# Layer 2's attention block: one store per head for the first block's turned sums, a fetch split by heads, and the last norm's offset added to x

## The chip, the core and the metric

The kernel runs on one core of one Trainium2 chip. The metric is the device time of one execution in microseconds (us). A core has five queues of instructions that matter here: TensorE (PE, matmuls, with its weight loads as PEld), VectorE (DVE), ScalarE (ACT), GpSimd (POOL) and SyncE (SP). SP computes nothing: it issues the DMA transfers. Each queue is worked through in order, and a queue stands while its first instruction waits.

## What is computed

The program is a network of four layers on x of shape (4, 128, 64, 64): four batches of 128 channels and 4096 positions. Layer 0 is a convolution with a state-space scan, layer 1 a 3x3 convolution, layer 2 an attention block and a mixture of experts, layer 3 a linear attention and another mixture of experts. The change lies in layer 2's attention block alone. Its reference, cut to what matters (`t` is x as 4096 tokens of 128 values, 16 heads of 8):

```python
def _L2_attn_ref(x, ...):
    qkv = _qz_ring(heads + rx_theta)              # products of cosines
    q = jnp.transpose(qkv, (0, 2, 1, 3))
    scores = jnp.einsum('bhsd,bhtd->bhst', q, q) / np.sqrt(D)
    attn = jax.nn.softmax(scores, axis=-1)
    ctx = jnp.einsum('bhst,bhtd->bhsd', attn, q)
    ...
    attn_out = ctx @ w_comb.T + b_comb
    x1 = _ln(x + attn_out, g1, beta1)
    zf = jnp.cos(x1[..., :NQ_FFN]) * jnp.cos(ry_theta)
    h = jax.nn.relu(zf @ w1.T + b1)
    ffn_out = h @ w2.T + b2
    return _ln(x1 + ffn_out, g2, beta2)
...
t = t + _L2_attn_ref(_ln_t(t), ...)
```

Queries, keys and values are one array, so the matrix of scores is symmetric.

## The kernel before

**Stages.** `layer2_attention` works on one batch after another. For batch b it runs a stage that mixes two jobs, `feed_forward(b - 1)` and `prepare(b)`, and then `attention(b)`. Before the first attention there is only a preparation, after the last only a feed-forward. So there are four attentions and four stages that hold a feed-forward. Between a stage and an attention the on-chip buffers are given up and taken anew: the first writes of the next stage can't start before the last readers of the old buffers are done.

**Order.** In `attention` the order on PE, DVE and POOL is the order in which the code is written. In the mixed stages the compiler's scheduler orders every queue, from its own estimates of durations; the order in the code is only a priority. `in_turn` gives that priority: in turn i it calls the last step for chunk i - 9, the step before it for chunk i - 8, and so on back to the first step for chunk i.

**Attention.** The 4096 queries are cut into four blocks j of 1024. Because of the symmetry, the exponentials of only some pairs of blocks are computed: block j meets the key blocks `meets[j]` from ((1, 2), (2, 3), (3,), (0,)), and its own. A pair's exponentials serve twice: upright in `weigh`, where PE sums them into `ctx_ps` for the queries of block j, and turned by DVE (L1401, L1425), where `turn` sums them into `accs[h][:, i]` for the queries of the met block i (L1309, L1311). For blocks 1 to 3 these turned sums are added into `ctx_ps` before `weigh` copies the block out (L1353) and stores numerators and denominators by head (L1358, L1359). Block 0 is finished first, while its turned sums come from block 3, at the head's end. They therefore go to memory on their own: `around_d`. On chip such a sum has 128 rows: row 32 g + 8 a + d is the g-th of four partial sums, for quarter a of each run of 128 tokens, and dimension d of the head. Columns are (t, r): token 128 t + 32 a + r. In L1315 to L1321 each of the sixteen groups of 8 rows (g, a) is stored by a DMA of its own, so that `around_d[g]` is in the order of dimensions and tokens.

**Feed-forward.** Ten steps per chunk of 512 tokens, in the order of chunks 2 to 7, then 0 and 1: `fetch` (loads of den, num, nrm_in, and for chunks 0 and 1 of `around`), `divisors`, `attended`, `first_centred`, `first_norm`, `cosines`, `hidden`, `sum_up`, `last_centred`, `last_norm`. `divisors` adds the four parts of `around` into num on POOL (L1465, L1466). `sum_up` also requests the x chunk (L1517), to which `last_norm` adds the block's result on POOL (L1534) before it is stored (L1535). x has three buffers. Both norms run through `layernorm_steps`: after the square on ACT (L105) come a matmul of means, a transpose, square root, reciprocal and transpose, a multiplication by the gain on DVE (L120) and the addition of the offset on POOL (L121). The buffer of `around` shares the tag "hid" with the hidden layer's, two buffers in all.

**Preparation.** `prepare` norms the chunk, stores it (`nrm_d`, L1131), computes the products of cosines on DVE, ACT and POOL (L1152, L1154, L1156), and stores values and heads (`value_d` L1170, `head_d` L1184). At its end `load(0)` issues 32 loads (L1097) of queries and keys for the first head, which POOL rounds (L1106).

Of the kernel before, what the change touches and what calls it, by code (L numbers as in the profile page):

```python
# [9 lines left out]
F32 = mybir.dt.float32  # L10
# [3 lines left out]
ALU = mybir.AluOpType  # L14
# [3 lines left out]
P = 128  # L18
NB = 4
HW = 64  # L20
L = HW * HW
CH = 512
# [7 lines left out]
class Common:  # L30
# [58 lines left out]
    def mm(self, out, lhsT, rhs, start=True, stop=True):  # L89
        self.nc.tensor.matmul(out, lhsT, rhs, start=start, stop=stop)  # L90
# [8 lines left out]
    def layernorm_steps(self, out, src, work, psum, g=None, b=None, tag="mm", bufs=None):  # L99

        nc = self.nc
        xc = psum.tile([P, CH], F32, name="ln_xc", tag=tag, bufs=bufs)
        self.mm(xc, self.center, src)
        sq = work.tile([P, CH], F32, name="ln_sq", bufs=bufs)
        nc.scalar.activation(sq, xc, AF.Square)  # L105
        yield
        vp = psum.tile([P, CH], F32, name="ln_var", tag="mm")
        self.mm(vp, self.mean, sq)
        vt = work.tile([P, CH // 32, 32], F32, name="ln_vt")
        nc.vector.transpose(vt.rearrange("p a b -> p (a b)"), vp)  # L110
        sd = work.tile([P, CH // 32, 1], F32, name="ln_sd")
        nc.scalar.activation(sd, vt[:, :, 0:1], AF.Sqrt, bias=self.eps5)
        nc.vector.reciprocal(sd, sd)
        rs = work.tile([P, CH // 32, 32], F32, name="ln_rs")
        nc.vector.transpose(rs, sd.to_broadcast([P, CH // 32, 32]))  # L115
        rs = rs.rearrange("p a b -> p (a b)")
        if g is None:
            nc.vector.tensor_tensor(out, xc, rs, ALU.mult)  # L118
        else:
            nc.vector.scalar_tensor_tensor(rs, xc, g, rs, ALU.mult, ALU.mult)  # L120
            nc.gpsimd.tensor_scalar(out, rs, b, None, ALU.add)  # L121
# [105 lines left out]
def column(nc, pool, v, name, n=1, p=P):  # L227

    t = pool.tile([p, n], F32, name=name)
    nc.sync.dma_start(out=t, in_=v.rearrange("(n p) -> p n", p=p))  # L230
    return t
# [786 lines left out]
def layer2_attention(K, xd, dpool, w):  # L1018

    nc, tc, mm = K.nc, K.tc, K.mm  # L1020
    NH, HD = 16, 8
    NJ = 4
    BT = NTT // NJ
    scale = 1.0 / math.sqrt(HD)
    with ExitStack() as ctx:
# [8 lines left out]
        g2 = column(nc, cst, w["g2"], "g2")  # L1034
        beta2 = column(nc, cst, w["beta2"], "beta2")
# [7 lines left out]
        for k in range(4):  # L1043
            r = slice(32 * k, 32 * k + HD)
# [29 lines left out]
        value_d = dpool.tile([NH, 32, NJ, 4, BT, HD], F32, name="value_d")  # L1074
        num_d = dpool.tile([2, P, L], F32, name="num_d")
        den_d = dpool.tile([2, NH, L], F32, name="den_d")
        around_d = dpool.tile([4, P, L // NJ], F32, name="around_d")
        nrm_d = [dpool.tile([P, L], F32, name=f"nrm_d{i}") for i in range(2)]

        unit = lambda p, c: slice(32 * (2 * p + c), 32 * (2 * p + c) + 32)  # L1080
# [118 lines left out]
        def attention(qt, first, dsum, big, two, work, pssc, psctx, psacc):  # L1199
# [56 lines left out]
            for k, (h, j, i) in enumerate(order):  # L1256
                at = fills[h, j, i][-1] + 3
# [20 lines left out]
            accs = {}  # L1278
# [4 lines left out]
            def turn():  # L1283

                r, h, j, i, td, sums = groups[0]
                if r == 0:
                    sums = groups[0][-1] = aps[:, halves[0] % 2]
                    halves[0] += 1
                groups[0][0] += 1
                tv = values[h, j]  # L1290
                for g in range(4):
                    n = 4 * r + g
                    q, t = divmod(n, BT)
                    at = 32 * (4 * t + q)
                    mm(
                        sums[32 * g : 32 * g + 32],
                        tv[:, n].rearrange("p a d -> p (a d)"),
                        td[:, :, at : at + 32],
                        start=r == 0,
                        stop=r == BT - 1,  # L1300
                    )
                if r < BT - 1:
                    return
                groups.pop(0)
                if h not in accs:
                    accs[h] = work.tile([P, NJ, BT, 32], F32, name="acc")
                at = accs[h][:, i]
                if j == from_[i][0]:
                    nc.vector.tensor_copy(at, sums)  # L1309
                else:  # L1310
                    nc.vector.tensor_tensor(at, at, sums, ALU.add)  # L1311
                if i == 0:


                    for g in range(4):  # L1315
                        for a in range(4):
                            rows_ = slice(32 * g + HD * a, 32 * g + HD * a + HD)
                            nc.sync.dma_start(
                                out=around_d[g, HD * h : HD * h + HD].rearrange("d (t a r) -> d t a r", a=4, r=32)[:, :, a],
                                in_=accs[h][rows_, 0],  # L1320
                            )  # L1321
                if i == meets[j][-1]:
                    waiting.append(now[0] + 2)

# [52 lines left out]
            for n, (h, j, m) in enumerate(steps):  # L1377
# [10 lines left out]
                i = m // 4  # L1388
# [16 lines left out]
                for _ in range(rounds[n]):  # L1405
                    turn()

                while folds and (folds[0][0] <= n and not behind or len(folds) > 5):
                    _, qs, at = folds.pop(0)
# [3 lines left out]
                if behind:  # L1413
                    sums = dacc[:, from_[i].index(j), h]
                for p in range(2):
                    ex = exs[:, p]
                    t = 2 * m + p
# [25 lines left out]
        def feed_forward(b, dsum, work, psum):  # L1443

            CHB = NCH // NJ
            loads, x1s, hids, sums, halves, lasts, rcs, arounds = {}, {}, {}, {}, {}, {}, {}, {}

            def fetch(c):
                cols = slice(c * CH, (c + 1) * CH)
                den = work.tile([2 * NH, CH], F32, name="den", bufs=3)  # L1450
                nc.sync.dma_start(out=den, in_=den_d[:, :, cols].rearrange("p h f -> (p h) f"))
                num = work.tile([P, 2, CH], F32, name="num", bufs=2)
                nc.sync.dma_start(out=num, in_=num_d[:, :, cols].rearrange("p q f -> q p f"))
                nrm = work.tile([P, CH], F32, name="nrm_in", bufs=4)
                nc.sync.dma_start(out=nrm, in_=nrm_d[b % 2][:, cols])
                if c < CHB:
                    part = arounds[c] = work.tile([P, 4, CH], F32, name="around", tag="hid")
                    nc.sync.dma_start(out=part, in_=around_d[:, :, cols].rearrange("g q f -> q g f"))
                loads[c] = num, den, nrm

            def divisors(c):
                num, den, at = loads[c]
                if c in arounds:
                    part = arounds.pop(c)
                    nc.gpsimd.tensor_tensor(part[:, 0:2], part[:, 0:2], part[:, 2:4], ALU.add)  # L1465
                    nc.gpsimd.tensor_tensor(num, num, part[:, 0:2], ALU.add)  # L1466

                tp = psum.tile([P, 4, 2 * NH], F32, name="den_t", tag="mm")
                for j in range(4):
                    nc.tensor.transpose(tp[:, j, :], den[:, j * P : (j + 1) * P], K.ident[0 : 2 * NH, 0 : 2 * NH])  # L1470
                rd = work.tile([P, 4, NH], F32, name="rd")
                nc.vector.tensor_reduce(rd, tp.rearrange("p j (z h) -> p j h z", z=2), AX.X, ALU.add)
                nc.vector.tensor_tensor(rd, rd, dsum[:, 4 * c : 4 * c + 4], ALU.add)
                nc.vector.reciprocal(rd, rd)
                rc = rcs[c] = work.tile([P, 4, NH, HD], F32, name="rc")
                nc.vector.tensor_copy(rc, rd.unsqueeze(3).to_broadcast([P, 4, NH, HD]))
# [36 lines left out]
                    nc.scalar.activation(hid[:, k, :], hps[k], AF.Relu, bias=b1[:, k : k + 1])  # L1513

            def sum_up(c):
                x = loads[c] = work.tile([P, CH], F32, name="x", bufs=3)
                nc.sync.dma_start(out=x, in_=xd[b][:, c * CH : (c + 1) * CH])  # L1517
                hid = hids[c]
                fp = psum.tile([P, CH], F32, name="ffn_ps", tag="mm")
                for k in range(4):  # L1520
                    mm(fp, w2T[:, k, :], hid[:, k, :], start=k == 0, stop=k == 3)
                r = sums[c] = work.tile([P, CH], F32, name="res")
                nc.vector.scalar_tensor_tensor(r, fp, b2, x1s[c], ALU.add, ALU.add)

            def last_centred(c):
                sums[c] = sums[c], work.tile([P, CH], F32, name="blk")
                lasts[c] = K.layernorm_steps(sums[c][1], sums[c][0], work, psum, g2, beta2, tag="xc", bufs=3)
                next(lasts[c])

            def last_norm(c):  # L1530
                next(lasts.pop(c), None)
                o = sums[c][1]
                x = loads[c]
                nc.gpsimd.tensor_tensor(x, x, o, ALU.add)  # L1534
                nc.sync.dma_start(out=xd[b][:, c * CH : (c + 1) * CH], in_=x)  # L1535
# [6 lines left out]
        for b in range(NB + 1):  # L1542
            with (
# [3 lines left out]
                with (  # L1547
# [4 lines left out]
                    if b < NB:  # L1552
                        part, qt, first = prepare(b, big, two, work, psum)
# [448 lines left out]
```

## Time and profile before

| what | us |
|---|---|
| median of 3 runs | 10257.94 (10254.08 to 10261.23) |
| the profiled execution's own time | 10257.22 |
| its span | 10255.4 |
| PE / DVE / ACT / POOL busy | 8783.8 / 7559.2 / 7455.2 / 4791.2 |
| layers 0 and 1, up to about | 2970 |
| attentions, about | 3116 to 4416, 4630 to 5934, 6149 to 7450, 7664 to 8950 |
| expert layers and layer 3, from about | 9100 |

The profile is one execution. A line of its timeline gives the start in us, the duration in us, the engine, the source line, the operation, and output<-input; x16 at the end means that sixteen such instructions in a row were merged. In square brackets stands how long the engine had been idle before it, and what ended the wait. SPq is SP's queue, where a DMA line is the issue, not the transfer. L90 is the helper through which nearly all matmuls are recorded, L110 to L121 are `layernorm_steps`, and L215 to L224 the cosine; for them the names of the tiles say which step it is. Over the whole span the DMA engines move 60 GB/s on average, and 193592 of the 631668 packets are under 512 B.

### The profile page before, as it was taken

Reading aid. Unit: us, or ns where it says so; the run is one execution under the profiler, and the core shown is the slowest. Engines: PE = TensorE matmul, PEld = TensorE weight load, DVE = VectorE, ACT = ScalarE, POOL = GpSimd, SP = SyncE. Lnnn points to the kernel's source line nnn. Section 1 sums busy time; section 2 is a strip of 40 time slices with the busy share of each in tenths; the row PEclk is TensorE's granted clock in tenths of the full one; section 3 lists DMA queues with packets and bytes.
Section 4 is the critical chain, followed back from the end, with each engine's and each line's share of the span. In section 5 each row is a group of like instructions: output and inputs, shape, how many; then the busy total and the mean of one; then the engine's idle time right before and its main releaser. Section 6 shows DMA issues by size and latency. Waiting matters only on the chain. (4 is left out here: it accounts for less than half of the span.)

```text
span 10255.4 us, 186421 instructions
## 1 busy us (share of the span) xinstructions
PE 8783.8 (86%) x72472; PEld 3322.6 (32%) x72472; DVE 7559.2 (74%) x8247; ACT 7455.2 (73%) x10632; POOL 4791.2 (47%) x3135
## 2 busy tenths in 40 slices
PE   6777777778868999979999969999969999967766
PEld 2222222224442333333333323333323333323433
DVE  1888788887846888877888868888868888753563
ACT  2666666664438999969999959999959999831531
POOL 1666676665524555545555545555545555420000
PEclk9787877888989999989999989999989999988988
DMA  3332423322212222232222132222142222123004
GB/s 81 98 79 69 103 68 97 76 61 73 79 62 48 38 39 39 37 98 42 40 39 42 32 104 38 40 43 39 29 111 35 42 38 40 34 95 117 0 18 148
DMA packets 631668, 617.44 MB, mean 60 GB/s; under 512 B 193592, under 2 KB 425088, under 8 KB 629760
## 3 DMA queue, kind: packets, MB, share of 16 engines
q1 hardware_dynamic: 630784, 605.51, 25.3%
q8 instruction: 572, 9.37, 0.4%
q14 instruction: 312, 2.56, 0.1%
HBM read 394.93 MB, written 91.23 MB: 47 GB/s over the span
## 5 line engine op out<-in xcount | busy, mean ns | idle before, releaser
L1419 ACT ACTIVATE ex<-score 128x1024 f32<-128x1024 f32 x5120 | 4927.2, 1037 | 175.0 <-PE score L90 89.5
L90 PE MATMUL ctx_ps<-ex,qt 128*32 128x512 f32 x20480 | 2735.0, 606 | 19.7 <-DVE ctx L1353 19.7
L1368 POOL TENSOR_TENSOR folded<-ex 128x1024 f32<-128x1024 f32 x512 | 1224.3, 2391 | 2123.2 <-ACT ex L1419 1853.4
L1425 DVE STREAM_TRANSPOSE turned<-ex 128x1024 f32<-128x1024 f32 x1536 | 1885.5, 1228 | 373.2 <-ACT ex L1419 295.8
L1401 DVE STREAM_TRANSPOSE turned<-ex 128x1024 f32<-128x1024 f32 x1532 | 1842.2, 1203 | 0.0
L90 PE MATMUL acc_ps<-turned,turned_v 128*32 128x256 f32 x24576 | 1769.5, 379 | 3.0 <-DVE turned L1431 3.0
L90 PE MATMUL score<-queries,keys 32*128 32x512 f32 x10240 | 1333.9, 497 | 93.8 <-ACT ex L1419 45.5
L829 DVE TENSOR_TENSOR_SCAN hs<-decay,carry,hs 128x512 f32<-128x512 f32 x1024 | 1246.0, 1264 | 181.7 <-ACT decay L825 167.7
L825 ACT ACTIVATE decay<-dt,a_neg 128x512 f32<-128x512 f32 x1024 | 692.8, 688 | 820.5 <-DVE hs L829 798.0
L90 PEld LDWEIGHTS acc_ps<-turned,turned_v 128*32 128x32 f32 x24576 | 800.9, 110 | 1476.4 <-issue 1327.1
L833 POOL TENSOR_TENSOR hs<-hs,c_sb 128x1024 f32<-128x1024 f32 x512 | 1209.4, 2362 | 60.5 <-DMA c_sb<-c_d 19.6
L90 PEld LDWEIGHTS score<-queries,keys 32*128 32x128 f32 x10240 | 512.6, 182 | 1190.5 <-ACT ex L1419 819.0
L1225 POOL TENSOR_TENSOR turned_v<-v,quarter 128x1024 f32<-128x1024 f32 x256 | 612.5, 2393 | 265.4 <-PE acc_ps L90 209.7
L90 PE MATMUL y_ps<-hs,pair 128*64 128x512 f32 x2048 | 673.2, 785 | 48.9 <-POOL hs L833 48.5
L818 DVE TENSOR_TENSOR hs<-dtx,b_ps 128x2048 f32<-128x2048 f32 x256 | 579.7, 2265 | 176.3 <-DMA dtx<-dtx 132.9
L1369 POOL TENSOR_TENSOR quarters<-folded 128x512 f32<-128x512 f32 x512 | 658.1, 1285 | 40.1
L90 PE MATMUL b_ps<-dbc,state 32*64 32x512 f32 x1024 | 342.8, 751 | 385.5 <-DVE hs L818 385.1
L90 PEld LDWEIGHTS ctx_ps<-ex,qt 128*32 128x32 f32 x20480 | 406.4, 108 | 654.7 <-issue 598.8
L832 POOL COPY carry<-hs 128x2 f32<-128x2 f32 x512 | 96.3, 188 | 897.0 <-DVE hs L829 847.0
L1419 ACT ACTIVATION_READ_ACCUMULATOR ex<-score 128x1 f32 x2048 | 437.2, 213 | 0.0
L1353 DVE COPY ctx<-ctx_ps 128x512 f32<-128x512 f32 x256 | 176.9, 691 | 328.9 <-PE ctx_ps L90 307.8
L1410 DVE TENSOR_REDUCE dacc<-quarters 128x2 f32<-128x512 f32 x508 | 327.0, 644 | 0.0
(358 smaller groups left out, 9384.2 us busy)
## 6 DMA issues: line engine op xcount, KB each, us to landing
c_sb<-c_d SPq DMA_DIRECT2D x512, 128.0 KB
queries<-head_d SPq DMA_DIRECT2D x1024, 64.0 KB
keys<-head_d SPq DMA_DIRECT2D x1024, 64.0 KB
dt<-dt SPq DMA_DIRECT2D x128, 256.0 KB
dtx<-dtx SPq DMA_DIRECT2D x128, 256.0 KB
v<-value_d SPq DMA_DIRECT2D x1024, 32.0 KB
w<-in_L_ffn_weight SPq DMA_DIRECT2D x32, 1024.0 KB
w<-in_L_ffn_weight SPq DMA_DIRECT2D x128, 256.0 KB
```

What stands on the lines that cost most here:

```text
L90: self.nc.tensor.matmul(out, lhsT, rhs, start=start, stop=stop)
L818: nc.vector.tensor_tensor(hs, dtx2, bb.unsqueeze(1).to_broadcast([P, NQ, CH]), ALU.mult)
L825: nc.scalar.activation(ex, dt2[:, q, :], AF.Exp, scale=a_neg[:, q, g : g + 1])
L829: nc.vector.tensor_tensor_scan(hs[:, q, :], decays[q - 2 * i], hs[:, q, :], carry[:, g, q : q + 1], ALU.mult, ALU.add)
L833: nc.gpsimd.tensor_tensor(hs[:, two, :], hs[:, two, :], cs.unsqueeze(1).to_broadcast([P, 2, CH]), ALU.mult)
L1225: nc.gpsimd.tensor_tensor(t, v.unsqueeze(2).to_broadcast([P, 4 * BT, 4, HD]), quarter.unsqueeze(1).to_broadcast([P, 4 * BT, 4, HD]), ALU.mult,
L1368: nc.gpsimd.tensor_tensor(hs, exs[:, :, 0], exs[:, :, 1], ALU.add)
L1369: nc.gpsimd.tensor_tensor(qs, hs[:, :, 0 : CH // 2], hs[:, :, CH // 2 :], ALU.add)
L1401: nc.vector.transpose(*upright)
L1410: nc.vector.tensor_reduce(at, qs, AX.X, ALU.add)
L1419: nc.scalar.activation(ex, sps[p], AF.Exp, scale=scale, accum_out=sums[:, t : t + 1] if summed else None)
L1425: nc.vector.transpose(*upright)
```

## The change

Four edits:

- In `turn`, the turned sums of block 0 are stored by one DMA per head, rows and columns as they stand on chip; `around_d` has a part for each head.
- In `fetch`, `around` is loaded by 16 DMAs, one per head, each to that head's 8 rows; the sixteen (g, a) groups now lie side by side in a row. `divisors` adds groups 8 to 15 onto 0 to 7, then each half of the result onto the matching half of num, whose columns are read and written in the order (a, t, r).
- `layernorm_steps` gets a third form: with a gain and no offset, DVE writes the product to the result, and POOL's addition is left out. The last norm uses it.
- The request of the x chunk goes from `sum_up` to `last_centred`, the next step, behind that step's own instructions, and POOL adds the offset beta2 to x there.

```diff
@@ layernorm_steps
         if g is None:
             nc.vector.tensor_tensor(out, xc, rs, ALU.mult)
+        elif b is None:
+            nc.vector.scalar_tensor_tensor(out, xc, g, rs, ALU.mult, ALU.mult)
         else:
@@ layer2_attention
-        around_d = dpool.tile([4, P, L // NJ], F32, name="around_d")
+        around_d = dpool.tile([NH, P, L // NJ // 4], F32, name="around_d")
@@ turn
                 if i == 0:
-                    for g in range(4):
-                        for a in range(4):
-                            rows_ = slice(32 * g + HD * a, 32 * g + HD * a + HD)
-                            nc.sync.dma_start(
-                                out=around_d[g, HD * h : HD * h + HD].rearrange("d (t a r) -> d t a r", a=4, r=32)[:, :, a],
-                                in_=accs[h][rows_, 0],
-                            )
+                    nc.sync.dma_start(out=around_d[h], in_=accs[h][:, 0].rearrange("p t r -> p (t r)"))
@@ fetch
-                    part = arounds[c] = work.tile([P, 4, CH], F32, name="around", tag="hid")
-                    nc.sync.dma_start(out=part, in_=around_d[:, :, cols].rearrange("g q f -> q g f"))
+                    part = arounds[c] = work.tile([P, 16, P], F32, name="around", tag="hid")
+                    for h in range(NH):
+                        nc.sync.dma_start(
+                            out=part[HD * h : HD * h + HD],
+                            in_=around_d[h, :, c * P : (c + 1) * P].rearrange("(n d) f -> d n f", d=HD),
+                        )
@@ divisors
-                    nc.gpsimd.tensor_tensor(part[:, 0:2], part[:, 0:2], part[:, 2:4], ALU.add)
-                    nc.gpsimd.tensor_tensor(num, num, part[:, 0:2], ALU.add)
+                    nc.gpsimd.tensor_tensor(part[:, 0:8], part[:, 0:8], part[:, 8:16], ALU.add)
+                    for i in range(2):
+                        at = num[:, i].rearrange("p (t a r) -> p a t r", a=4, r=32)
+                        more = part[:, 4 * i : 4 * i + 4].rearrange("p a (t r) -> p a t r", r=32)
+                        nc.gpsimd.tensor_tensor(at, at, more, ALU.add)
@@ sum_up
-                x = loads[c] = work.tile([P, CH], F32, name="x", bufs=3)
-                nc.sync.dma_start(out=x, in_=xd[b][:, c * CH : (c + 1) * CH])
@@ last_centred
-                lasts[c] = K.layernorm_steps(sums[c][1], sums[c][0], work, psum, g2, beta2, tag="xc", bufs=3)
+                lasts[c] = K.layernorm_steps(sums[c][1], sums[c][0], work, psum, g2, tag="xc", bufs=3)
                 next(lasts[c])
+                x = loads[c] = work.tile([P, CH], F32, name="x", bufs=3)
+                nc.sync.dma_start(out=x, in_=xd[b][:, c * CH : (c + 1) * CH])
+                nc.gpsimd.tensor_scalar(x, x, beta2, None, ALU.add)
```

## The prediction

> **What bounds the kernel now.** I read, in this order, the page's costliest groups, the busy time by stage, and the timeline where one stage of layer 2's attention hands over to the next.
>
> ```profile
> L1419 ACT ACTIVATE ex<-score 128x1024 f32<-128x1024 f32 x5120 | 4927.2, 1037 | 175.0 <-PE score L90 89.5
> 3116.00:4416.00 1300.00, 1280.68 (x14586) 451.37 (x14586) 1038.40 (x1057) 1236.96 (x1792) 676.39 (x352) 0.99 0.21 37
> 4416.00:4630.00 214.00, 138.26 (x422) 63.62 (x422) 153.42 (x288) 117.39 (x173) 95.26 (x102) 0.81 0.42 122
> ```
>
> The first line is the exponential, 4927 us over four batches. The other two are one batch's attention and the stage behind it (columns: window, length, busy time and count of PE, weight loads, DVE, ACT, POOL; clock; DMA share; GB/s). In attention ACT works 1237 of 1300 us. Its waits in that window are 22.9 us on PE's scores, 11.7 us without a recorded cause and 3.6 us on POOL; none is on a DMA. The stores of the turned sums are therefore hidden while attention runs, and taking them away there brings nothing. In the 214 us stage no engine is near full (PE 138, DVE 153): it is a chain of waits with idle ends. The four feed-forward stages are where the change acts. This is the end of attention 0:
>
> ```profile
> 4403.21 0.42 DVE L1309 COPY acc<-acc_ps 128x256 f32<-128x256 f32 x1 [3.29 <-PE acc_ps L90]
> 4403.66 11.53 SPq L1318 DMA_DIRECT2D around_d<-acc  x16
> 4404.26 1.86 DVE L1441 TENSOR_REDUCE dsum<-dacc 128x512 f32<-128x1024 f32 x1
> 4416.78 0.33 SPq L1451 DMA_DIRECT2D den<-den_d  x1
> 4419.20 0.60 PE L1470 MATMUL den_t<-ident,den 32*128 32x32 f32 x4 [16.06 <-DMA den<-den_d]
> 4424.87 0.60 ACT L105 ACTIVATE ln_sq<-ln_xc 128x512 f32<-128x512 f32 x1 [27.98 <-DMA nrm_in<-nrm_d]
> ```
>
> The last head's turned sums are copied at 4403.2. SP then issues sixteen stores in 11.5 us, and the first load of the next stage (den) leaves only at 4416.78; the view of SP's waits gives its last 1.3 us to "DMA around_d<-acc". Compute is done at 4406.1 (DVE dsum), yet PE idles 16.06 us and ACT 27.98 us. Nothing covers this gap.
>
> The other end of the stage, where attention 1 starts:
>
> ```profile
> 4616.24 6.11 SPq L1535 DMA_DIRECT2D xd<-x  x3
> 4623.11 0.45 SPq L1517 DMA_DIRECT2D x<-xd  x1
> 4626.75 1.26 POOL L1534 TENSOR_TENSOR x<-x,blk 128x512 f32<-128x512 f32 x1 [4.75 <-DMA x<-xd]
> 4628.04 0.32 SPq L1535 DMA_DIRECT2D xd<-x  x1
> 4630.40 1.28 ACT L1419 ACT_TABLE_LOAD   x1 [15.61 <-DMA xd<-x]
> ```
>
> The eighth x chunk is requested at 4623.11, because its buffer is free only after an earlier chunk's store, and SP stands in three stores until 4622.35. It arrives, is added at 4626.75, stored at 4628.04, and ACT, idle for 15.61 us, starts when that store has landed. Last, what follows a fetch:
>
> ```profile
> 3081.71 11.04 SPq L1097 DMA_DIRECT2D keys<-head_d  x16
> 3099.77 1.89 POOL L1106 CAST keys<-keys 128x2048 fp32r<-128x2048 f32 x1 [21.23 <-DMA queries<-head_d]
> ...
> 9015.66 0.37 SPq L1458 DMA_DIRECT2D around<-around_d  x1
> 9020.78 2.36 POOL L1465 TENSOR_TENSOR around<-around 128x1024 f32<-128x1024 f32 x1 [3.80 <-DMA around<-around_d]
> ...
> 4501.21 1.60 POOL L1484 TENSOR_TENSOR num<-num 128x512 f32<-128x512 f32 x1
> 4538.09 0.64 DVE L1485 TENSOR_TENSOR num<-num,rd_ps 128x512 f32<-128x512 f32 x1
> ```
>
> Sixteen 64 KB key loads of 8 partitions in 512 B rows, which is exactly the new fetch's form, are usable 18.1 us after the first issue; today's single 1 MB fetch is usable 5.1 us after its issue here (6.4 us in the first fetch of that stage, 8.4 us at 4519.55). In the last pair the chunk that needs the first fetch is ready on POOL at 4502.8, and DVE takes it up at 4538.1.
>
> **What the Trainium skill says.** "DMA: Bandwidth & Descriptors", section "Why a DMA increments its semaphore by 16 and not by 1": a DMA runs on as many engines, up to 16, as divide the slowest dimension of both sides; 8 partitions get at most 8. The trace agrees in direction: 68 GB/s over the key loads (3081.7 to 3099.8), 253 GB/s over the stretch after the fetch at 4489.1. [...] The x store at 4628.04 releases ACT 2.36 us later, its issue included[...]. "GPSIMD Engine Reference", section "Performance pitfalls for Q7 kernels": reads slow down when the inner step passes 8 bytes. The new adds step 4 bytes in runs of 32, so I price them like today's; no row of before has that form.
>
> **The change, part by part.** The sum is against the profiled execution, 10257.2 us (span 10255.4), which is within 1 us of the median 10257.9.
>
> 1. *Stores.* 1024 issues become 64. In attention, hidden as said: 0. At the four ends, from first store to first den load: 4403.66 to 4416.78 = 13.1; 5919.54 to 5932.19 = 12.65; 7438.67 to 7451.18 = 12.5; 8953.97 to 8966.70 = 12.7; together 51.0 us. Now one store takes about 0.35 to issue (head_d's, of 128 partitions too, 0.38) and 2.0 to land, like the x store. DVE's dsum ends 2.46 us after the first store, so both finish together and each gap shrinks to 2.5. Gain 51.0 - 10.0 = 41 us. Late next is den's own load (2.4 us, as now). If the store lands late like the 3.6 us x load, the gain is 36.
>
> 2. *Fetch by heads.* Per batch two fetches; each puts 16 issues on SP (keys: 11.04 us) in place of one (0.43), and the data comes 18.1 instead of 5 to 8 us after the first issue: 10 to 13 us later, 11.5 taken. Behind them on SP wait head_d, value_d and nrm_d stores, and in the last batch den, nrm_in and expert weights; each then leaves up to 10.6 us late. Behind the waiting add on POOL wait num's sums and the next cosine product (L1152) or norm offset (L121), and DVE and PE behind those. Lower bound 0: DVE takes the two chunks 35 us (4502.8 to 4538.1) and 32 us (4534.7 to 4566.6) after POOL has them, and in the last batch 13 and 17 us (9017.0 to 9030.1, 9028.4 to 9045.6). If the compiler's order puts other POOL work first, it is hidden. Upper bound 11.5 each. The order is laid from the compiler's own estimates, and the trace says how it sees this form: it placed the casts of loaded keys on POOL at 4611.3, 18 us after SP's issues end at 4593.0 and after another chunk's L121. It takes such loads as slow, so it will plan around them. I take 1.5 us each, 8 x 1.5 = 12.
>
> 3. *POOL adds.* 128x1024 add kept (2.35); L1466 (2.54) becomes two of 128x512 (1.27 each): 0. A fixed cost of 0.2 more would be 16 x 0.2 = 3 at most, inside the slack above.
>
> 4. *Offset.* The 32 L121 adds on blk (1.65) leave the chain between the norm and the x add, and 32 adds of the same shape on x come in: POOL's total stays. DVE's L120 keeps its 0.74, with another target. The new add is hidden where x waits in its buffer; on the last chunk it isn't. At the last stage's end:
>
> ```profile
> 9094.61 1.56 POOL L121 TENSOR_SCALAR blk<-ln_rs,beta 128x512 f32<-128x512 f32 x1 [0.21 <-DVE ln_rs L120]
> 9096.26 1.26 POOL L1534 TENSOR_TENSOR x<-x,blk 128x512 f32<-128x512 f32 x1
> 9099.61 2.67 SPq L1941 DMA_DIRECT2D x<-xd  x4
> ```
>
> there x is long present (requested 9084.46), so 1.65 us go.
>
> 5. *x one step later, with 4.* At the three starts of attention everything depends on the request at 4623.11. If it stays there, the offset is added after it lands: 1.56 us lost each. If the earlier adds no longer wait for L121, the three stores move up. The last norm's L120 runs end at 4609.6, 4613.75 and 4616.7; the third store then goes at about 4618.2, the request at 4619.2, x lands at 4622.9 (3.64 as now), offset 1.56, add 1.26, store: ACT at 4628.2, a gain of 2.2. If the request goes right after the buffer's own store, each add waits only for its norm: last store at 4618, ACT at 4620.3, a gain of 10. Between 2.2 and 10 I take 4: 12 us in three.
>
> Sum: -41 + 12 + 0 - 1.65 - 12 = -43, so 10257 - 43 = 10214 us.
>
> **Rivals.** *A, the forecast:* gap closed, fetch mostly hidden. Own range 10195 to 10235 (fetch 0 to 3 us each, starts 0 to 8 each). Chance 0.58.
> *B, half-exposed fetch:* the wait moves from the store to the fetch. For it: POOL already stood 3.80 us for a fetch at 9020.78, and 7.4 us in all. Against: the 35 us of slack. At 6 us each, 48 in place of 12: 10214 + 36 = 10250. Chance 0.19.
> *C, starts clear fully:* 10 us at each of three starts, fetch at 1 us: -41 + 8 - 1.65 - 30 = -65, 10192. For it: two of three stores at 4616 wait on adds that need no L121 any more. Against: SP still issues 32 key and query loads ahead of the x stores. Chance 0.10.
> *D, slower:* the around add keeps its place on POOL (ahead of L1152 or L121), and every engine's queue stands until the data lands, 11.5 us in eight places: 92 us, -55 + 92 = +37, 10294. It decides above (54.65 + 20.5) / 8 = 9.4 us exposed per fetch. The trace's slack and the casts' late place speak against it, its in-order POOL waits for it. Chance 0.13.
> *The change doesn't do what it says:* if den's load waited for something other than the stores, part 1 would be lost. The named wait and DVE's end at 4406.1 leave no candidate; I give it nothing of its own.
>
> **Numbers.** About 0.2%, 20.5 us, is what can be told from no change here: faster is below 10237, slower above 10278. A and C are faster (0.68), B is no change (0.19), D slower (0.13). The predicted time is A's, 10214. The range takes in A, most of C and B: 10188 to 10262, leaving out D and the outer edges.
>
> **What would show it.** Right: one L1318-like store per head, and about 2.5 us instead of 13 from it to den; ACT's first wait in the stage near 18 us, not 28. Fetch hidden: POOL's wait at the around add under 3 us each, with L121 or L1152 ahead of it. Wrong if that wait is near 10 us and DVE's wait beside it grows alike, or if ACT's 15.6 us at the starts of attention grows. Attention itself should keep its 1300 us; a change of more than 3 us there would be a cause that I haven't seen.

## The result and the profile after

The change made the kernel slower: 10355.11 us median of 5 runs (10348.50 to 10362.34) against 10257.60 (10253.53 to 10261.23) before, a ratio of 1.0095 with a 95% interval of 1.0081 to 1.0108. The profiled execution's span is 10353.3 us.

The group of the exponentials on the page, and the same two stretches of time as before the change (columns: window, length, busy time and count of PE, weight loads, DVE, ACT, POOL; clock; DMA share; GB/s):

```profile
L1415 ACT ACTIVATE ex<-score 128x1024 f32<-128x1024 f32 x5120 | 4927.7, 1037 | 174.9 <-PE score L90 87.7
```

```profile
3122.00:4422.00 1300.00, 1285.99 (x14602) 455.07 (x14603) 1040.68 (x1062) 1238.84 (x1794) 679.13 (x354) 0.99 0.22 39
4422.00:4663.00 241.00, 142.28 (x407) 62.95 (x406) 148.63 (x283) 113.10 (x169) 91.85 (x102) 0.76 0.38 97
```

Attention is as it was, 1300 us with ACT busy for 1239. The mixed stage behind it takes 241 us in place of 214, with hardly more work on any engine: PE 142 for 138, DVE 149 for 153. The loss is idle time. I measure it from here on as a *gap*, from the end of an attention's last exponential to the start of the next attention's first one:

| | gap 1 | gap 2 | gap 3 | last attention to the next layer's x loads |
|---|---|---|---|---|
| before | 234.9 | 237.7 | 234.0 | 152.5 |
| after | 262.6 | 262.4 | 265.4 | 163.3 |

The four differences are 27.7, 24.7, 31.4 and 10.8, together 94.6 of the 97.9 us by which the spans differ. Of the rest, +6.0 lies ahead of the first attention, whose first exponential starts between 3114.8 and 3123.8 us in all fourteen traces, and -3.0 behind the last.

**The end of attention 0.** This is the timeline of the kernel after:

```profile
4409.02 0.35 SPq L1317 DMA_DIRECT2D around_d<-acc  x1
4409.62 1.86 DVE L1437 TENSOR_REDUCE dsum<-dacc 128x512 f32<-128x1024 f32 x1
4411.08 0.31 SPq L1447 DMA_DIRECT2D den<-den_d  x1
4413.48 0.60 PE L1473 MATMUL den_t<-ident,den 32*128 32x32 f32 x4 [4.97 <-DMA den<-den_d]
4419.49 0.60 ACT L105 ACTIVATE ln_sq<-ln_xc 128x512 f32<-128x512 f32 x1 [17.25 <-DMA x_in<-xd]
```

One store of 0.35 us stands where sixteen took 11.53. The den load follows 2.06 us after the store (13.1 before), PE idles 4.97 us (16.06), ACT 17.25 (27.98). This part did what it says.

**The fetch by heads.** The timeline again, with the loads and the adds of both fetches:

```profile
4486.49 9.14 SPq L1455 DMA_DIRECT2D around<-around_d  x16
...
4513.48 9.87 SPq L1455 DMA_DIRECT2D around<-around_d  x16
...
4529.83 1.93 POOL L123 TENSOR_SCALAR x<-ln_rs,beta 128x512 f32<-128x512 f32 x1 [9.97 <-DVE ln_rs L122]
4534.61 0.30 POOL L1154 TENSOR_TENSOR q<-cs 128x64 f32<-128x64 f32 x1 [2.85 <-ACT cs L226]
4534.99 2.17 POOL L1156 TENSOR_TENSOR q<-q,cs 128x64 f32<-128x64 f32 x5
4537.14 2.34 POOL L1465 TENSOR_TENSOR around<-around 128x1024 f32<-128x1024 f32 x1
...
4577.19 2.33 POOL L1465 TENSOR_TENSOR around<-around 128x1024 f32<-128x1024 f32 x1
```

No bracket stands at either add: POOL never waits for the fetch. Yet the adds stand 50.7 and 63.7 us behind their first load. In the kernel before it was 7.2 and 8.4 us:

```profile
4489.14 0.43 SPq L1458 DMA_DIRECT2D around<-around_d  x1
...
4496.30 2.34 POOL L1465 TENSOR_TENSOR around<-around 128x1024 f32<-128x1024 f32 x1
...
4519.55 0.43 SPq L1458 DMA_DIRECT2D around<-around_d  x1
...
4527.93 2.35 POOL L1465 TENSOR_TENSOR around<-around 128x1024 f32<-128x1024 f32 x1 [0.75 <-DMA around<-around_d]
```

The order itself has changed: between the first load and its add POOL now carries out 29 instructions in both fetches, where it carried out 8 and 7 before.

Was the data late by that much? In the kernel after, the same stretch by windows (columns as above; the last two are DMA share and GB/s):

```profile
4505.00:4510.00 5.00, 5.00 (x13) 2.04 (x12) 5.00 (x12) 0.83 (x2) 2.35 (x2) 1.00 0.00 0
...
4530.00:4537.00 7.00, 3.57 (x10) 2.19 (x10) 2.19 (x6) 4.83 (x6) 3.76 (x7) 0.50 0.00 0
```

From 4505 to 4510 the DMA engines move nothing, so the first fetch is in by 4505, at most 18.5 us after its first issue. From 4530 to 4537 they move nothing again, so the second is in by 4530, at most 16.5 us after its first issue. Until 4529.83 POOL stands for 9.97 us at a norm offset that the order puts ahead of the first add, with that add's data lying ready.

**The start of attention 1**, in the timeline:

```profile
4602.68 11.10 SPq L1099 DMA_DIRECT2D keys<-head_d  x16
4614.01 13.19 SPq L1099 DMA_DIRECT2D queries<-head_d  x15
4629.01 0.32 SPq L1531 DMA_DIRECT2D x<-xd  x1
4658.42 1.56 POOL L1532 TENSOR_SCALAR x<-x,beta 128x512 f32<-128x512 f32 x1 [4.21 <-DMA x<-xd]
4660.06 1.26 POOL L1538 TENSOR_TENSOR x<-x,blk 128x512 f32<-128x512 f32 x1
4661.35 0.32 SPq L1539 DMA_DIRECT2D xd<-x  x1
4663.45 1.28 ACT L1415 ACT_TABLE_LOAD   x1 [32.98 <-DMA xd<-x]
```

The last x store leaves at 4661.35, after four more rounds of request, offset, add and store behind the loads of keys and queries. ACT idles 32.98 us (15.61 before).

So two suspects remain: the place of the sum in the order, and the chain of x. Theory 1 is the place, a *planned* delay. Theory 2 is the x chain. Theory 3, the old rival D, is a fetch that lands late; the missing waits speak against it.

### The profile page after: what moved, and what is told of

It reads as the page before. It is cut to its first block, busy times and chain, and to the rows that moved or that the text cites. A ratio compares the mean times of both kernels' runs of the same rounds, so it can differ in the third digit from the quotient of the medians.

```text
span 10353.3 us, 185669 instructions
## 1 busy us (share of the span) xinstructions
PE 8815.7 (85%) x72472; PEld 3329.1 (32%) x72472; DVE 7550.7 (73%) x8247; ACT 7446.1 (72%) x10624; POOL 4789.3 (46%) x3143
```

## The experiments

All are against the kernel before, timed beside it on the same chip; there its median was 10258.2 to 10259.3 us (10257.6 beside the kernel after), so the runs can be compared with one another. "Gaps" is the mean change of the three gaps against before (235.5).

| kernel | median us | ratio, 95% interval | gaps |
|---|---|---|---|
| stores_only | 10220.27 | 0.9961 (0.9948 to 0.9974) | -8.9 |
| x_only | 10246.47 | 0.9987 (0.9981 to 0.9994) | -2.4 |
| fetch_only | 10357.45 | 1.0094 (1.0079 to 1.0109) | +25.0 |
| no_x | 10304.64 | 1.0043 (1.0026 to 1.0060) | +12.3 |
| fetch4 | 10259.29 | 0.9997 (0.9988 to 1.0006) | -0.5 |
| fetch16w | 10247.58 | 0.9990 (0.9981 to 0.9998) | -3.8 |
| fetch_w32 | 10280.55 | 1.0021 (1.0013 to 1.0030) | +8.0 |
| fetch_w16 | 10318.42 | 1.0057 (1.0042 to 1.0072) | +18.5 |
| early | 10225.73 | 0.9972 (0.9960 to 0.9983) | -11.9 |
| after_x4 | 10301.87 | 1.0043 (1.0028 to 1.0058) | +10.1 |
| repack_x | 10220.38 | 0.9961 (0.9947 to 0.9976) | -11.9 |
| repack_x4 | 10197.93 | 0.9939 (0.9924 to 0.9954) | -21.3 |

**The parts one by one.** Stores alone, on the kernel before:

```diff
-                    for g in range(4):
-                        for a in range(4):
...
+                    nc.sync.dma_start(
+                        out=around_d[h // 4, :, (h % 4) * 256 : (h % 4) * 256 + 256],
+                        in_=accs[h][:, 0].rearrange("p t r -> p (t r)"),
+                    )
```

> Kernel before with one edit: a head's turned sums are stored by one DMA of 128 partitions in place of 16, and fetched with the old single load; so block 0's turned sums are added at wrong places, and nothing else differs. All theories: the first wait at the end of each attention falls from about 28 to about 17 us, the gap between attentions shrinks by about 10.5, the time goes to about 10216. If the stores had a hidden price, it would be above 10240.

The fetch alone, on the kernel before:

```diff
-                    nc.sync.dma_start(out=part, in_=around_d[:, :, cols].rearrange("g q f -> q g f"))
+                    for h in range(NH):
+                        nc.sync.dma_start(
+                            out=part[HD * h : HD * h + HD],
+                            in_=around_d[:, HD * h : HD * h + HD, cols].rearrange("g q f -> q g f"),
+                        )
```

> Kernel before with one edit: the turned sums of a chunk are fetched by 16 loads of one head each into the old layout, all else old, x too. Theory 1 (the order of instructions, laid down before the run, puts the sum with the turned sums and all behind it late because of the 16 loads, though their data is long there): the add stands 50 us or more behind the first load, POOL idles little at it, and each gap grows by about 30, the time to some 10370 to 10400. Theory 2 (the x request and its offset cost the time): 10257, no gap grows by over 3. Theory 3 (the loads really land late): POOL idles 10 us or more at the add, by 10300.

x alone is the change's edits of `layernorm_steps`, `sum_up` and `last_centred` on the kernel before; no_x is the kernel after with the edits of `sum_up` and `last_centred` taken back.

> Kernel before with one edit: x requested one step later and given the norm's offset beforehand on POOL; stores and fetch old. Theory 1: within 15 us of 10257 and gaps within 3 us of the old. Theory 2: each gap grows by 25 to 35, the time to 10370 to 10400, with POOL idle at each offset for 3 us or more.

> Kernel after with x as before: requested in the step ahead, the offset added behind the norm; stores by heads and fetch by heads stay. Theory 1: about as slow as after, 10340 to 10360. Theory 2: 10216, all of the loss gone. A division of the loss between both would lie between, and with x_only and fetch_only the parts should add up to after.

Stores alone gain 39.0 us, about as expected. x alone gains 12.8. The fetch alone loses 98.2, and its add has no wait either. That is theory 1's sign and mechanism, but less than the 10370 to 10400 us and the 30 us in each gap that it expected. Its second fetch in the timeline:

```profile
4522.80 10.14 SPq L1459 DMA_DIRECT2D around<-around_d  x16
...
4587.61 2.33 POOL L1469 TENSOR_TENSOR around<-around 128x1024 f32<-128x1024 f32 x1
```

But theory 1 doesn't cover all: no_x lies 50.5 us below after, where theory 1 expected 10340 or more. The same x edit that gains 12.8 us beside the old fetch costs 50.5 beside the new one. Theory 2 is wrong of the edit by itself. Of the pair it covers about half: it expected no_x at 10216, with all of the loss gone.

**What makes the fetch late: number or width?** Two cuttings of the load, on the kernel before, both of 128 partitions:

```diff
@@ fetch4
+                    for g in range(4):
+                        nc.sync.dma_start(out=part[:, g], in_=around_d[g, :, cols])
@@ fetch16w
+                    for g in range(4):
+                        for k in range(4):
+                            at = slice(k * P, (k + 1) * P)
+                            nc.sync.dma_start(out=part[:, g, at], in_=around_d[g, :, c * CH + k * P : c * CH + (k + 1) * P])
```

> Kernel before with one edit: the turned sums of a chunk are fetched by 4 loads of 128 partitions (one per partial sum) in place of one. If the order is planned as though the loads of one queue followed one another at some 2.5 to 3 us each, 4 of them are ready 12 us after the first: the add stands 10 to 20 us behind the first load, inside the slack, no gap grows by over 5, 10250 to 10275. If any cutting of this load costs, whatever the count, gaps grow by 20 or more, 10340 or over.

> Kernel before with one edit: the same bytes by 16 loads of 128 partitions and 128 columns each, so each transfer runs at full width and only the count is that of after. Count theory (the planned order counts loads): as fetch_only, the add 45 us or more behind the first load, gaps +20 to +27, 10340 to 10360. Width theory (loads to 8 partitions are slow, or are held to be): near before, the add within 20 us of the first load, 10250 to 10280.

I had thought that the number of loads was counted. It isn't: sixteen wide loads cost nothing, and with four the add stands 7.9 us behind the first (4490.21 to 4498.07), not the 10 to 20 that I had expected. In the timeline of fetch16w:

```profile
4494.90 7.85 SPq L1461 DMA_DIRECT2D around<-around_d  x16
...
4504.65 2.34 POOL L1468 TENSOR_TENSOR around<-around 128x1024 f32<-128x1024 f32 x1 [2.56 <-DMA around<-around_d]
```

The add stands 9.8 us behind the first load, so early that POOL does wait 2.56 us for the data. SP's occupation by sixteen issues is thereby cleared too: they take 7.85 us here (9.14 in after) and nothing is lost.

Then the width was varied, on the kernel before, with 4 loads of 32 partitions and 8 of 16:

```diff
+                    for k in range(4):
+                        rows_ = slice(32 * k, 32 * k + 32)
+                        nc.sync.dma_start(out=part[rows_], in_=around_d[:, rows_, cols].rearrange("g q f -> q g f"))
```

> Kernel before with one edit: the turned sums of a chunk are fetched by 4 loads of 32 partitions each. If the plan prices a load by the bytes of one partition, so that k narrow loads of one queue cost k times the one wide load (16 of them some 50 us), 4 cost some 12 us: the add stands 10 to 20 us behind the first load, within the slack of 32 us, and the time stays at 10250 to 10275. If narrowness alone costs, gaps grow by 10 or more, over 10300.

> Kernel before with one edit: 8 loads of 16 partitions each. By the same price 8 loads take some 25 us: the add stands 22 to 32 us behind the first load, at the edge of the slack, gaps grow by 0 to 10, 10250 to 10300. If the price doesn't go by the number of narrow loads, it equals the loss of 16 loads of 8 partitions, 10340 to 10360.

The second fetch of the same stage, first in fetch_w32 and then in fetch_w16:

```profile
4528.02 1.85 SPq L1460 DMA_DIRECT2D around<-around_d  x4
...
4563.27 2.34 POOL L1467 TENSOR_TENSOR around<-around 128x1024 f32<-128x1024 f32 x1
```

```profile
4518.21 4.40 SPq L1460 DMA_DIRECT2D around<-around_d  x8
...
4576.18 2.33 POOL L1467 TENSOR_TENSOR around<-around 128x1024 f32<-128x1024 f32 x1
```

| loads of the second fetch | POOL instructions from first load to add (7 before) | us from first load to add | later than before (8.4) | beyond the 32 us of slack | gaps grew by |
|---|---|---|---|---|---|
| 4 of 32 partitions | 18 | 35.2 | 26.8 | none | 8.0 |
| 8 of 16 | 29 | 58.0 | 49.6 | 17.6 | 18.5 |
| 16 of 8 (fetch_only) | 29 | 64.8 | 56.4 | 24.4 | 25.0 |

The width decides. The four loads of fetch_w32 are as many and as large as those of fetch4, with rows of the same 2 KB; only the partitions differ, and the gaps grow by 8.0 us where they had changed by -0.5. The sixteen of fetch_only and fetch16w are alike in number and bytes (their rows differ, 2 KB and 512 B), and the gaps change by +25.0 and -3.8.

For the two narrowest forms the delay of the add, less the slack that I had read in the kernel before, is the growth of the gap to within 1 us. Both expectations failed, though. For 32 partitions the add was to stand 10 to 20 us behind and the time to stay; it rose by 21 us. For 16 the add was to stand 22 to 32 us behind, with 10300 us at most; it stands 58.0 behind, and the time is 10318. A price in proportion to the number of narrow loads is thus wrong: 4, 8 and 16 of them put the add 26.8, 49.6 and 56.4 us later.

What the trace shows for 32 partitions is three waits of ACT, 15.3 us in all, whose releaser is this add: the hidden layer's buffers, which `around` shares, come free late. That it makes up the 8 us of each gap was not tried.

**Is it the place, or the loads themselves?** The kernel after, with the same 32 narrow loads, requested in the second turn of the stage, and chunks 0 and 1 taken fourth and fifth:

```diff
@@ fetch, with the loads by heads taken out of the branch for c < CHB
+                if c == CHB + 1:
+                    for k in range(CHB):
+                        part = arounds[k] = work.tile([P, 16, P], F32, name="around", tag="hid")
+                        for h in range(NH):
+                            nc.sync.dma_start(
+                                out=part[HD * h : HD * h + HD],
+                                in_=around_d[h, :, k * P : (k + 1) * P].rearrange("(n d) f -> d n f", d=HD),
+                            )
@@ order
-            order = [*range(CHB, NCH), *range(CHB)]
+            order = [2, 3, 4, 0, 1, 5, 6, 7]
```

> Kernel after with its 16 loads of 8 partitions kept, but requested in the second turn of the stage for both chunks, and chunks 0 and 1 taken as fourth and fifth in place of last (both buffers are free then). If the loss comes from the place that the late loads give the sum in the order, it goes: 10205 to 10235. If 16 loads of 8 partitions cost by their issues or transfers, wherever they stand, 32 issues of 0.7 us and the loads behind them hold the first chunks: 10290 or more.

```profile
4411.50 18.14 SPq L1457 DMA_DIRECT2D around<-around_d  x32
...
4435.43 4.65 POOL L1466 TENSOR_TENSOR around<-around 128x1024 f32<-128x1024 f32 x2
```

All 32 narrow loads are issued in 18.14 us and the sums are made 23.9 us after the first, in the timeline above. The loss is gone: 129 us below after, with every narrow load, new add and x edit of it kept; the early request and the order of the chunks are the differences. So the loads cost little by issues or bytes; they cost where the end of the stage hangs on a sum that the order places late. Little is not nothing: in the last stage POOL waits 10.09 us at the first of the two adds for these loads.

Two things this run leaves open. It doesn't place the sum late either: POOL carries out 9 instructions from the first of 32 loads to the add, against 29 for 16 loads in after. So a narrow load has no fixed price; where the sum lands depends on what else there is to place. And whether the early request or the new order of the chunks is the cure was not separated.

**What the x edit adds.** One more buffer for x, on the kernel after:

```diff
-                x = loads[c] = work.tile([P, CH], F32, name="x", bufs=3)
+                x = loads[c] = work.tile([P, CH], F32, name="x", bufs=4)
```

> Kernel after with one edit: x has four buffers in place of three. At the start of an attention x goes through fetch, offset, add and store one chunk after another because its buffers are taken. If that chain is the part of the loss that appears only when both parts of the change are there (about 50 us over four stages), gaps shrink by 5 or more at the three starts, 10310 to 10340. If what holds it is SP's 32 loads ahead of it, no change: 10345 to 10360.

The groups of instructions (columns: count, busy us, mean ns, then idle time ahead of them and what ended it), in the kernel after:

```profile
L1532 POOL TENSOR_SCALAR x<-x,beta 128x512 f32<-128x512 f32 x32 | 50.0, 1566 | 57.2 <-DMA x<-xd 57.2
L120 DVE SCALAR_TENSOR_TENSOR blk<-ln_xc,g,ln_rs 128x512 f32<-128x512 f32 x32 | 24.0, 751 | 46.0 <-POOL x L1538 45.0
```

and with four buffers:

```profile
L1532 POOL TENSOR_SCALAR x<-x,beta 128x512 f32<-128x512 f32 x32 | 50.4, 1582 | 19.4 <-DMA x<-xd 19.4
L120 DVE SCALAR_TENSOR_TENSOR blk<-ln_xc,g,ln_rs 128x512 f32<-128x512 f32 x32 | 24.0, 751 | 17.8 <-POOL x L1538 16.5
```

In the kernel after, POOL idles 57.2 us for x, and DVE, which now writes `blk` itself, 45.0 us for the add that frees its buffer. POOL's wait alone is no sign of the loss, as it is 44.2 us in x_only too, which gains. DVE's is: in x_only its idle time at that line is 1.1 us. With the fourth buffer both waits shrink, and 53 us of time with them (10301.87, somewhat more than expected).

The start of attention 1 shows the chain. Behind SP's loads of keys and queries stand five adds of x (L1538; L1537 in no_x). From the first to the last they take 22.8 us in after and 11.6 us in no_x, where the offset is no part of the chain. This is ACT's first row of attention 1 in no_x:

```profile
4649.64 1.28 ACT L1415 ACT_TABLE_LOAD   x1 [20.19 <-DMA xd<-x]
```

So behind SP's loads three buffers bind. That the late sum is what crowds the last chunks there is argued: the fourth buffer was not tried without the x edit, and it is worth 22 us without the late sum too, as the next runs show. That leaves about 31 of the 53 us for the late sum.

**A version that beats both.** One DMA from memory to memory per head puts the rows in order, so that a chunk is fetched by a single load of 128 partitions; the rest is the kernel after. `again` is called for head h - 1 beside head h's store, and for the last head behind the first chunk's loads:

```diff
+        def again(h):
+            nc.sync.dma_start(
+                out=again_d[:, HD * h : HD * h + HD],
+                in_=around_d[h].rearrange("(n d) f -> n d f", d=HD),
+            )
@@ fetch
+                    nc.sync.dma_start(out=part, in_=again_d[:, :, c * P : (c + 1) * P].rearrange("n q f -> q n f"))
```

> Kernel after with one edit: each head's part of the turned sums is put in the order of rows by one DMA from memory to memory, issued with the next head's store (the last one behind the first loads of the next stage), and a chunk is fetched by one load. If the 16 loads are the cause of the loss, this keeps the gains of the stores (-39) and of x (-13): 10205 to 10215, adds within 15 us of their load. If the head layout or the new adds cost by themselves, 10260 or more. If the moves from memory to memory delay the first loads of the stage, between.

With four buffers for x as well:

> The variant with one reordering move per head and one load per chunk, and x with four buffers in place of three. If x's buffers bind the start of an attention there too, 3 us or more less at each start: 10200 to 10212. If they bound only behind the late sum, no change from the variant with three: 10215 to 10225.

The timeline of the last:

```profile
4411.37 0.48 SPq L1443 DMA_DIRECT2D again_d<-around_d  x1
...
4486.96 0.43 SPq L1463 DMA_DIRECT2D around<-again_d  x1
...
4494.12 2.63 POOL L1472 TENSOR_TENSOR around<-around 128x1024 f32<-128x1024 f32 x1
...
4613.21 1.28 ACT L1418 ACT_TABLE_LOAD   x1 [5.48 <-DMA xd<-x]
```

The add is back at 7.2 us behind its load, and the start of attention waits 5.48 us (13.00 with three buffers). With three buffers the time is 10220, with four 10198: the buffer is worth 22 us even without the late sum, more than I had expected.

repack_x lies a little above its expected 10205 to 10215, and no lower than stores alone (10220.38 against 10220.27). What x brings beside the faster stores can't be read from this pair, because the moves from memory to memory differ too: the three gaps are 3 us shorter each than with stores alone, but ACT's first wait behind attention 0 is 20.38 us against 17.04.

## Why the prediction was wrong

It said 10214 us, and the kernel takes 10355.

1. *Stores*, -41: right, in size and by the path that was named. stores_only gives -39.0, and the ACT wait named as evidence, near 18 us, is 17.25.
2. *Fetch by heads*, +12: **this step failed.** "It takes such loads as slow, so it will plan around them. I take 1.5 us each." The fetch alone costs 98.2 us, 12.3 for each of the eight. I had looked at the sign that mattered, the place of the casts, and drew comfort from it. I had also read it too small: the issues that end at 4593.0 are those of the queries. The loads that the first cast needs are those of the keys, and in the kernel before it stands 41 us behind the first of them:

```profile
4570.12 11.36 SPq L1097 DMA_DIRECT2D keys<-head_d  x16
...
4611.26 1.89 POOL L1106 CAST keys<-keys 128x2048 fp32r<-128x2048 f32 x1
```

An order that believes loads to be slow moves other work ahead of the sum; but all that hangs on the sum goes back with it, and chunks 0 and 1 are the last of the stage. The slack of 32 us bore out for the two narrowest forms. I held it against the landing, 18.1 us (itself an upper bound, as the row shown for it names a load of queries as the releaser), instead of against the delay that the order would give: 56.4 us for the second fetch in fetch_only, of which 24.4 stick out. The upper bound of 11.5 bounded the wrong quantity for the same reason.
3. *POOL adds*, 0: right. Each half takes 1.26 us, two for the old 2.54.
4. and 5. *Offset and x*, -13.65 together: right alone in the sum, -12.8 in x_only. That its size fits so well is in part luck: the three gaps shrink by 5.2 and 3.2 us and grow by 1.2, 7.2 us in all for the 12 forecast. Taking them as a sum with the rest was the second error: beside the late sum they cost 50.5. The bound of 1.56 us lost per start came from the last request alone. But the offset enters every round that runs behind SP's loads: in after five requests stand there (4629.01 to 4654.59), and ACT starts after a wait of 32.98 us, against 20.19 in no_x.

In sum: stores -39.0, fetch on top of them +84.4 (10304.64 - 10220.27), x on top of both +50.5, together +95.9. These three steps lead from before to after, so they add up by themselves; the measured 97.5 differs only because the kernel before has another median there. The parts tried alone, -39.0, +98.2 and -12.8, would give +46.4.

Rival D had the right sign and a like size for the fetch (92 us), by a mechanism that the runs exclude: engines waiting at the add until data lands. At its eight adds POOL idles 0 us in after. My own test, "POOL's wait at the around add under 3 us" as proof of a hidden fetch, was met while the fetch was exposed. A view of waits can't show a delay that is already in the order.

What stays open is why the order puts the sum so late. The estimates behind it are not in a trace; that it believes narrow loads to be slow is inferred from where the add stands. The Trainium skill's "DMA: Bandwidth & Descriptors", section "Why a DMA increments its semaphore by 16 and not by 1", lets a load of 8 partitions run on at most 8 engines. The traces agree in direction: the engines move 94 GB/s while sixteen narrow loads run (4488 to 4497 in after) and 143 while sixteen wide ones do (4496 to 4504 in fetch16w). But by the same rule loads of 32 and of 16 partitions get 16 engines, as one of 128 does, and their adds were placed late all the same. So that rule doesn't account for the place of the add.

## What to carry to other kernels

Where a compiler orders the engines, a new form of load can cost by where the order places its user, and not only by what the load takes: look up an old row of that form, see how far behind its own first load its user is placed, and hold that against the slack. After a change, look beside the waits for data that lies ready: DMA share 0, no bracket at the user, and more instructions than before between load and use. And try two edits of one stage together: a buffer count that is enough for each may bind for both.

## What the runs showed of the hardware

- Sixteen loads of 64 KB to 128 partitions deliver 1 MB little later than a single load: the add waits for them and stands 9.8 us behind the first issue, against 7.2 us with one load.
- A narrow load's issue can be short (0.26 us is the median of the 128 in after), but sixteen take 9.14 us. In both fetches of the first stage together, SP waits 5.8 us between them for earlier loads of `around` to land.
- POOL's add over columns in the order (a, t, r), runs of 32 elements, takes 1.26 us for 128x512, as a plain one does (1.27).
- A reordering move from memory to memory of 128 KB costs SP 0.48 us, and an attention with fifteen of them keeps its length (1281.6 us from first to last exponential in repack_x4, 1281.4 before).
